# Loads at the start, banks of the hidden sums, and the order of the last outer product in a Strassen FFN kernel

## The chip, the cores and the metric

The kernel runs on one core of one Trainium2 chip. The metric is the device time of a run in microseconds; three runs of the kernel before gave a median of 1380.54 us (1380.38 to 1381.13). One further execution was recorded by the hardware profiler; its trace and the page made from it are what is read here. The engines are PE (TensorE, with its weight loads as PEld), DVE (VectorE), ACT (ScalarE), POOL (GpSimd) and SP (SyncE, which issues most transfers).

## What is computed

```python
def cond(x, condition, weights):           # x (32, 64, 1024)
    W = weights[condition]                 # (32, 64, 64), gathered
    return jnp.einsum('bct,bcd->bdt', x, W)

def ffn(input, inter_w, inter_b, output_w, output_b):   # D = 1024, F = 4096
    h = gelu(jnp.einsum('bsd,df->bsf', input, inter_w) + inter_b)
    return jnp.einsum('bsf,fd->bsd', h, output_w) + output_b

x = x + ffn(cond(x, itok_B_0_15, cond_weights), ...)
```

All of it is in fp32. The 32 rows of x are first mixed with a small matrix each, which is picked by an index; the result goes through two large matrix products with a gelu between, and x is added at the end.

## The kernel before

**Two levels of Strassen.** Each of the two large products is done by a Strassen-Winograd scheme of two levels. Layer one ("f") has eight iterations `it`, each with seven outer products; layer two ("z") has seven outer products `o` (`OUTER`, order 1, 2, 6, 7, 4, 5, 3), each with seven middle products (`MID`, order 1, 2, 5, 6, 4, 7, 3). Each of these blocks is seven inner products (`INNER`), which are issued as matmuls of 128x256 and accumulate in PSUM. One inner product is eight matmul records.

**PSUM.** Pool `pst` has two buffers of one bank (tag "t"). Pool `psacc` has tags A, B and C, two buffers each. In a block the inner products come in slots: 0 in A, 1 in B, 2 in C, 3 in A, 5 in C, 6 in A and 11 (that is, slot 4 of the next block) in A. VectorE reads each product and adds it to running sums in SBUF (`add`, line 181).

**The order is written by hand.** Every piece of work is entered as `at(time, function, ...)`, and the list is issued in the order of these times. One unit is one inner product; a block takes 7 units and an iteration or outer product 49. Each engine runs its instructions in the order of issue.

**Start.** x comes in pairs of rows, 16 in all; ten of them are mixed at the start and six later. `FIRST = (2, 3, 6, 7, 0, 1, 4, 5)` and then 8 and 9 is the order. `load_x` issues a load on SP (line 275), `gather` fetches the small matrices with POOL, `mix` runs 16 small matmuls (32 records, tile py, line 308), and `mixed` copies py to SBUF by ScalarE (L331) and VectorE (L333). xpool has six buffers. The last two of `FIRST`, 4 and 5, go to a buffer of another pool. On SP the loads stand in the order x2, x3, x6, x7, w11, x0, x1, x4, x5, w12, x8, x9, w21, w22, b1, where wij is a quarter of 1 MB of the first layer's weights. POOL makes sums of the weights (wi, ws) from them, and VectorE sums of y. Before the first mix, `warm` runs matmuls on zeros.

**After gelu.** From iteration 4 on, `hidden` also makes sums of the four parts of a gelu result. For the inner ones `inner_s1_copy` copies half of a part to PSUM by ScalarE (`to_psum`, L200), and `inner_s1` adds it by VectorE. The PSUM tile is of tag "B", which fB uses in slot 1 of each block. There are 16 such hidden blocks with four copies each.

**The last outer product.** In layer two, `product3` and `read3` do the inner products and their additions to the middle sums mD, mX, mY, mZ (`MID_STATE`). A result that is done (`MID_DONE`) goes to the outer sums, is transposed by PE (tile tp, L1006), added to x (`load_xb`, L996) and stored (`store_out`, L1017). `mid_w`, `mid_h`, `mid_s3`, `inner_w2` and `inner_h2` prepare operands on POOL and VectorE ahead of each block. In outer product 6, which is the last, the results of the last middle products go straight to the output, by `add_copy`, `ends_in` and the transposes.

Of the kernel before, what the change touches and what calls it, by code (L numbers as in the profile page):

```python
# [9 lines left out]
F32 = mybir.dt.float32  # L10
# [53 lines left out]
}  # L64
MID_DONE = {2: (("D", (0, 0)),), 7: (("X", (1, 1)), ("Y", (1, 0))), 3: (("Z", (0, 1)),)}
MID_SUM = 6


@with_exitstack
def kernel(  # L70
# [101 lines left out]
    def at(time, fn, *args):  # L172
        steps.append((time, len(steps), fn, args))
# [20 lines left out]
    def to_psum(src, tag=None):  # L194
        uid[0] += 1
        pool = late["acc"] if tag else pst
        t = pool.tile([P, 2, W], F32, tag=tag or "t", name=f"t{uid[0]}")
        if len(src.shape) == 2:
            t = t.rearrange("p k n -> p (k n)")[:, : src.shape[1]]
        nc.scalar.copy(t, src)  # L200
        return t

# [63 lines left out]
    FIRST = (2, 3, 6, 7, 0, 1, 4, 5)  # L266

    def load_x(i):
        if i in FIRST[6:]:
            if "x" not in XT:  # L270
                XT["x"] = misc.tile([P, 2, T], F32, tag="m8", name="x0_m")
            XT[i] = XT["x"][:, FIRST.index(i) - 6, :]
        else:
            XT[i] = xpool.tile([P, T], F32, tag="x0", name=f"x0_{i}")
        nc.sync.dma_start(XT[i], x_rows[i])

    def warm():
# [276 lines left out]
    S1 = {}  # L554

    def inner_s1_copy(it, fin, sub):
        S1[it, fin, sub] = to_psum(H[it, fin, sub][:, 1, :], "B")

    def inner_s1(it, fin, sub):

# [113 lines left out]
    t0 = -len(order) * MIX - 0.7  # L674
    for j, i in enumerate(order):
        t = t0 + j * MIX
        at(-40 + 0.1 * j if j < 8 else t0 + (j - 6) * MIX + 1.5, load_x, i)
        at(t, mix, i)
        at(t + MIX + 0.4, mixed, i)
    at(t0 + 10 * MIX + 1, store_y1, 8)  # L680
    at(-39.65, load_w1, 0, "11")
    at(-38, load_w1, 0, "12")
    at(t0 + 3 * MIX + 1.7, load_w1, 0, "21")
    at(t0 + 3 * MIX + 1.8, load_w1, 0, "22")
    at(-1, lambda: nc.sync.dma_start(b1, inter_b.rearrange("(f p) -> p f", p=P)))
    at(t0 + 10 * MIX + 0.42, end_mix)
    ty = t0 + 4 * MIX + 1.5
# [24 lines left out]
    for it in range(nit):  # L712
        a, s = divmod(it, NG)
        b0 = 49 * it
        if it > 0:
            for n, t in W_LOAD.items():
                at(b0 - 49 + t, load_w1, it, n)
        for n, t in W_AT.items():
            if it == 0:
                t = {1: -10, 2: -8, "s3": -4, "s1": -3}.get(n, t)  # L720
            if isinstance(n, str):
                at(b0 + t, outer_w1, it, n)
            else:
                at(b0 + t, inner_w1, it, n)
        for o, p in enumerate(OUTER):
            b = b0 + 7 * o
            plan_block(
                b, 1, 7 * it + o, (it, p), "f", mm1,
                lambda l, r, it=it, p=p, a=a: (WI[it, p][l], YI[a, p][r]),
            )  # L730
            fin = STATE[p][1]
            if fin is not None:
                hidden(b, it, fin)
            if it == NG:
                at(b - 49 + 13, load_y1, Y_ORDER[o])
                right_sums(b - 49 + 20, lambda p=p: inner_y(1, p), gap=0.8)
        pieces = []
        if it == 1:
            for k in range(KQ):
                e = {}  # L740
                t = b0 + 5 + 10.8 * k
                at(t, load_piece, k, e)
                right_sums(t + 5, lambda k=k, e=e: piece_targets(k, e), gap=0.8)
                at(t + 10.5, store_piece, k, e)
        elif it >= 2:
            n = -(-len(w2_pieces) // (nit - 2))
            for j in range(n):
                i = (it - 2) * n + j
                if i < len(w2_pieces):
                    e = {}  # L750
                    t = b0 + 9.5 + 14 * j
                    pc = w2_pieces[i]
                    at(t - 6, load_w2, pc, e)
                    at(t - 2.5, early_t1, pc, e)
                    at(t + 0.6, store_w2, pc, e, ("11", "21", "22"))
                    right_sums(t, lambda pc=pc, e=e: w2_targets(pc, e), gap=0.8)
                    at(t + 5, store_w2, pc, e, ("t1", "t2", "t3", "t4"))
# [55 lines left out]
    def mid_s3(time, o, t):  # L813

        e = {}

        def one(k):
            if k == 0:
                HT[o, "s3", t] = yq.tile([P, NG, 2, W], F32, tag="yq", name=f"hs3_{o}_{t}")
            e[k] = to_psum(HT[o, "s2", t][:, k])  # L820

        def two(k):
            add(nc.vector, HT[o, "s3", t][:, k], HT[o, "22", t][:, k], e[k], sub=True)

        for k in range(NG):
            at(time + 0.8 * k, one, k)
            at(time + 0.8 * k + 0.6, two, k)
# [35 lines left out]
    def inner_h2(time, o, q):  # L863
# [15 lines left out]
        for k in range(2):  # L879
# [4 lines left out]
            at(t + 1.9, sub, "s4", "12", "s2", k)  # L884
            at(t + 2.2, sub, "s3", "22", "s2", k)

    MS = {}
    OS = {}
    b2c = lambda n2, n1, n0: late["b2"][:, 4 * n2 + 2 * n1 + n0 : 4 * n2 + 2 * n1 + n0 + 1]
# [1 line left out]

    def product3(o, i, r):
        _, p, bank, start, _ = r
        q = MID[i]
        if start:
            acc3[o, i, bank] = late["acc"].tile(
                [P, 2, W], F32, tag=bank, name=f"z{bank}{o}{i}"
            )[:, 0, :]
        mm3(acc3[o, i, bank], win(o, q, RIGHT[p]), hin(o, q, LEFT[p]), start)
# [6 lines left out]

    def read3(o, i, r):
        _, _, bank, _, (t, n0) = r
        q = MID[i]
        acc = acc3[o, i, bank]  # L910
        for tgt, src in MID_STATE[q]:
            first = (o, i, tgt, t, n0) not in seen
            seen.add((o, i, tgt, t, n0))
            m = pair(o, tgt, t)[:, n0, :]
            if first and src is None:
                nc.scalar.copy(m, acc)  # L916
            elif first:
                add(nc.vector, m, acc, MS[o, src, t][:, n0, :])
            else:
                add(nc.vector, m, acc, m)  # L920
# [93 lines left out]
    def store_out(o, blk, t, n0s=(0, 1), eng=nc.sync):  # L1014
# [19 lines left out]
    )  # L1034
    for o in range(7):
        b = end1 + 49 * o
        pick = lambda later, first: b + (first if o == 0 else later)
        for (n, t), tt in H_LOAD.items():
            at(pick(*tt), load_h, o, n, t)
        for n, tt in W_LOAD2.items():  # L1040
            at(pick(*tt), load_w, o, n)
        for n, k, *tt in POOL2:
            if n == "w":
                at(pick(*tt), inner_w2, o, MID[k])
            elif n[0] == "t":
                at(pick(*tt), mid_w, o, n)
            else:
                at(pick(*tt), mid_h, o, n, k)
        mid_s3(b + 24, o, 0)
        mid_s3(b + 28, o, 1)  # L1050
        for i, q in enumerate(MID):
            bq = b + 7 * i
            inner_h2(bq - 2.2 if (o, i) != (0, 0) else bq + 0.7, o, q)
            rs = INNER
            if (o, i) == (6, 6):

                at(bq + 7.01, read3, o, i, (6, 7, "A", False, (1, 0)))
                rs = INNER[:-1] + ((7, 4, "B", True, (1, 0)),)
            for r in rs:
                at(bq + r[0], product3, o, i, r)  # L1060
                at(bq + r[0] + 1, read3, o, i, r)
            if q == MID_SUM:
                for t in range(2):
                    add_copy(
                        bq + (7.1, 12.1)[t],
                        lambda o=o, t=t: MS[o, "Z", t], lambda o=o, t=t: MS[o, "X", t],
                    )
            for j, (src, mb) in enumerate(MID_DONE.get(q, ())):
                for t in range(2):
                    if (o, i) == (6, 6):  # L1070

                        add_copy(
                            bq + (1.2, 4.45)[t],
                            lambda o=o, t=t: MS[o, "Z", t],
                            lambda mb=mb, t=t: OS["X", mb, t],
                        )
                        at(bq + 6.3, ends_in, o, mb, t)
                    f = bq + (7.1, 12.2)[t] + j
                    if (o, i) != (6, 6):
                        at(f, outer_copy, o, src, mb, t)  # L1080
                        at(f + 0.7, outer3, o, src, mb, t)
                    if STATE[OUTER[o]][1] is None:
                        continue
                    at(b + 38 if (o, mb, t) in ENDS else f - 1.8, load_xb, o, mb, t)
                    if (o, i) == (6, 6):
                        continue
                    at(f + 2.2, transpose, o, mb, t)
                    at(f + 3.2, add_x, o, mb, t)
                    at(f + 4, store_out, o, mb, t)
# [52 lines left out]
```

## Time and profile before

| | |
|---|---|
| runs, median of 3 | 1380.54 us (1380.38 to 1381.13) |
| profiled execution, time | 1380.57 us |
| profiled execution, span | 1378.8 us |
| mean granted clock of TensorE | 0.985 |
| bytes moved by DMA | 273.40 MB, mean 198 GB/s |

Busy times on the page are sums over one execution. An engine's "idle before" is time in which it stood still before instructions of a group, and the name behind the arrow is what released it. A granted clock of 0.5 means that TensorE ran at half speed. A few matmul records can be missing from a trace. Names such as fA or zB are the PSUM tiles of the two layers by bank; fD, fV and fX are sums in layer one, mX, mY and mZ in layer two.

### The profile page before, as it was taken

Reading aid. Unit: us, or ns where it says so; the run is one execution under the profiler, and the core shown is the slowest. Engines: PE = TensorE matmul, PEld = TensorE weight load, DVE = VectorE, ACT = ScalarE, POOL = GpSimd, SP = SyncE. Lnnn points to the kernel's source line nnn. Section 1 sums busy time; section 2 is a strip of 40 time slices with the busy share of each in tenths; the row PEclk is TensorE's granted clock in tenths of the full one; section 3 lists DMA queues with packets and bytes.
Section 4 is the critical chain, followed back from the end, with each engine's and each line's share of the span. In section 5 each row is a group of like instructions: output and inputs, shape, how many; then the busy total and the mean of one; then the engine's idle time right before and its main releaser. Section 6 shows DMA issues by size and latency. Waiting matters only on the chain.

```text
span 1378.8 us, 18997 instructions
## 1 busy us (share of the span) xinstructions
PE 1353.6 (98%) x6568; PEld 1184.9 (86%) x6568; DVE 883.4 (64%) x1579; ACT 487.5 (35%) x984; POOL 961.4 (70%) x601
## 2 busy tenths in 40 slices
PE   9999999999999999999999999999999999999998
PEld 8988888888888788788788888888888888888886
DVE  1656557575687755756657575675766757767675
ACT  1533324234254442532524332432333333333241
POOL 7462854958659477496672985958959689595791
PEclk7799999999999999999999999999999999999999
DMA  8255578686897757676668327074270723907511
GB/s 285 71 169 200 172 224 285 215 279 223 285 358 267 247 189 252 228 229 223 227 206 294 111 92 290 19 292 163 89 278 3 285 103 112 357 28 268 204 51 57
DMA packets 135216, 273.40 MB, mean 198 GB/s; under 512 B 15440, under 2 KB 67920, under 8 KB 123472
## 3 DMA queue, kind: packets, MB, share of 16 engines
q1 hardware_dynamic: 134336, 271.53, 57.0%
q8 instruction: 53, 0.87, 0.3%
q0 software_dynamic: 512, 0.53, 0.1%
q14 instruction: 43, 0.35, 0.1%
q10 hardware_dynamic: 272, 0.13, 0.0%
HBM read 167.28 MB, written 104.86 MB: 197 GB/s over the span
## 4 chain that ended last, share of the span: by engine, by line
PE 92%; DVE 4%; ACT 1%; issue 1%; DMA 1%; POOL 0%; DVEq 0%; ACTq 0%
PE fA L525 26%; PE zA L536 23%; PE fC L525 13%; PE zC L536 12%; PE fB L525 7%; PE zB L536 6%; PE py L308 2%; DVE hs L181 1%; PE tp L1006 1%; PE warm L286 1%; PE pl L308 1%; ACT t L200 1%; DMA y<-y_d 1%; DVE fX L181 1%; DVE fV L181 1%
## 5 line engine op out<-in xcount | busy, mean ns | idle before, releaser
L525 PE MATMUL fA<-yi,wi 128*128 128x256 f32 x896 | 212.5, 380 | 2.2 <-DVE fD L181 0.8
L181 DVE TENSOR_TENSOR hs<-h,t 128x512 f32<-128x512 f32 x308 | 199.8, 678 | 7.1 <-ACT t L200 3.4
L536 PE MATMUL zA<-hs,wt 128*128 128x256 f32 x840 | 198.1, 379 | 0.0
L181 POOL TENSOR_TENSOR h<-h,h 128x1024 f32<-128x1024 f32 x84 | 196.1, 2361 | 0.6 <-DMA h<-hs_d 0.6
L525 PEld LDWEIGHTS fA<-yi,wi 128*128 128x128 f32 x896 | 169.4, 190 | 27.7 <-DVE fX L181 1.9
L536 PEld LDWEIGHTS zA<-hs,wt 128*128 128x128 f32 x840 | 158.6, 190 | 20.9
L181 POOL TENSOR_TENSOR ws<-w,w 128x1024 f32<-128x1024 f32 x32 | 74.8, 2360 | 75.2 <-PE fA L525 75.1
L550 ACT ACTIVATE fD<-fD,b 128x256 f32<-128x256 f32 x128 | 57.9, 500 | 187.5 <-DVE fD L181 186.7
L181 POOL TENSOR_TENSOR wi<-w 128x512 f32<-128x512 f32 x80 | 101.7, 1271 | 30.5 <-PE fC L525 24.6
L200 ACT COPY t<-h 128x512 f32<-128x512 f32 x140 | 81.9, 590 | 82.4 <-DVE hs L181 78.2
L200 ACT COPY t<-hs 128x512 f32<-128x512 f32 x112 | 65.4, 588 | 113.6 <-DVE hs L181 113.6
L181 POOL TENSOR_TENSOR wt<-v 128x512 f32<-128x512 f32 x35 | 44.5, 1272 | 82.2 <-DMA v<-w_d 78.4
L181 DVE TENSOR_TENSOR fX<-fA,fX 128x512 f32<-128x512 f32 x104 | 71.3, 685 | 47.0 <-PE fA L525 46.7
L181 POOL TENSOR_TENSOR wi<-w,wi 128x512 f32<-128x512 f32 x40 | 50.8, 1271 | 61.7 <-PE fA L525 55.0
L525 PE MATMUL fC<-y,wi 128*128 128x256 f32 x384 | 91.0, 380 | 0.1
L525 PEld LDWEIGHTS fC<-y,wi 128*128 128x128 f32 x384 | 72.7, 190 | 10.4 <-issue 0.5
L536 PE MATMUL zC<-hs,v 128*128 128x256 f32 x336 | 79.5, 379 | 1.3 <-ACT mX L916 1.3
L536 PE MATMUL zA<-h,wt 128*128 128x256 f32 x328 | 77.5, 379 | 0.0
L525 PE MATMUL fA<-yi,w 128*128 128x256 f32 x320 | 75.6, 379 | 0.0
L536 PEld LDWEIGHTS zC<-hs,v 128*128 128x128 f32 x336 | 63.8, 190 | 10.3 <-ACT mX L916 1.7
L525 PE MATMUL fB<-y,w 128*128 128x256 f32 x256 | 63.6, 393 | 7.9 <-DVE fV L181 7.9
L536 PEld LDWEIGHTS zA<-h,wt 128*128 128x128 f32 x328 | 62.3, 190 | 8.5
(178 smaller groups left out, 2820.6 us busy)
## 6 DMA issues: line engine op xcount, KB each, us to landing
h<-hs_d SPq DMA_DIRECT2D x56, 1024.0 KB, 6.9
w<-in_L_ffn_inter_w_dram SPq DMA_DIRECT2D x32, 1024.0 KB, 6.7
hs_d<-hs SPq DMA_DIRECT2D x96, 256.0 KB, 3.1
v<-w_d SPq DMA_DIRECT2D x21, 1024.0 KB, 10.8
hs_d<-fD SPq DMA_DIRECT2D x64, 256.0 KB, 5.7
w2p<-in_L_ffn_output_w_dram SPq DMA_DIRECT2D x32, 512.0 KB, 5.7
w_d<-w2p SPq DMA_DIRECT2D x64, 256.0 KB, 2.8
w_d<-w2t SPq DMA_DIRECT2D x48, 256.0 KB, 6.6
```

Of the source, the lines that this page charges most:

```text
L181: eng.tensor_tensor(o, a, b, ALU.subtract if sub else ALU.add)
L200: nc.scalar.copy(t, src)
L286: nc.tensor.matmul(t[:, :W], z[:, :P], z[:, P:], start=True, stop=True)
L308: nc.tensor.matmul(out[j][:, k, :], XT[i][half, ts(k, P)], wsel(i)[half, :], start=True, stop=True,)
L525: nc.tensor.matmul(acc[:, u, :], lt[:, k, ts(u, P)], rt[:, k, :], start=start and u == 0 and k == 0, stop=k == 1, skip_group_check=True,)
L536: nc.tensor.matmul(acc, wl[:, k, :], hr[:, k, :], start=start and k == 0, stop=k == NG - 1, skip_group_check=True,)
L550: nc.scalar.activation(t[:, u, :], t[:, u, :], AF.Gelu_apprx_tanh, bias=b1[:, f : f + 1])
L1006: nc.tensor.transpose(tp[:, v, ts(n0, P)], d[:, n0, ts(v, P)], late["ident"])
```

## The change

It has three parts.

1. At the start, all ten x tiles come from xpool. Six x loads and w11 (after them) are issued first. The loads of pairs 4, 5, 8 and 9 follow when the mixes of 2, 3, 6 and 7 have freed a buffer; w12, w21 and w22 are issued after those. `inner_w1(0, 2)` gets a later time.
2. The copies of gelu's sums use tag "C" in place of "B".
3. In outer product 6 the middle products come in the order 1, 2, 5, 6, 7, 4, 3, with a state E in place of X for the result (1, 1). `mid_s3` is about five units earlier, POOL's work has an order of its own, one addition after middle product 6 is split in two, one operand tile (hs3_(6,1)) comes from another pool, and the loads of x and the last additions are earlier.

```diff
+MID_END = (1, 2, 5, 6, 7, 4, 3)
+MID_STATE_END = {**MID_STATE, 7: (("E", "Z"), ("X", "X")), 4: (("X", "X"),)}
+MID_DONE_END = {
+    2: (("D", (0, 0)),), 7: (("E", (1, 1)),), 4: (("X", (1, 0)),), 3: (("Z", (0, 1)),),
+}
...
     def load_x(i):
-        if i in FIRST[6:]:
-            if "x" not in XT:
-                XT["x"] = misc.tile([P, 2, T], F32, tag="m8", name="x0_m")
-            XT[i] = XT["x"][:, FIRST.index(i) - 6, :]
-        else:
-            XT[i] = xpool.tile([P, T], F32, tag="x0", name=f"x0_{i}")
+        XT[i] = xpool.tile([P, T], F32, tag="x0", name=f"x0_{i}")
         nc.sync.dma_start(XT[i], x_rows[i])
...
     def inner_s1_copy(it, fin, sub):
-        S1[it, fin, sub] = to_psum(H[it, fin, sub][:, 1, :], "B")
+        S1[it, fin, sub] = to_psum(H[it, fin, sub][:, 1, :], "C")
...
-        at(-40 + 0.1 * j if j < 8 else t0 + (j - 6) * MIX + 1.5, load_x, i)
+        at(-40 + 0.1 * j if j < 6 else t0 + (j - 6) * MIX + 1.5, load_x, i)
...
-    at(-39.65, load_w1, 0, "11")
-    at(-38, load_w1, 0, "12")
-    at(t0 + 3 * MIX + 1.7, load_w1, 0, "21")
-    at(t0 + 3 * MIX + 1.8, load_w1, 0, "22")
+    at(-39.45, load_w1, 0, "11")
+    for j, n in enumerate(("12", "21", "22")):
+        at(t0 + 3 * MIX + 1.6 + 0.1 * j, load_w1, 0, n)
...
-                t = {1: -10, 2: -8, "s3": -4, "s1": -3}.get(n, t)
+                t = {1: -10, 2: -6.8, "s3": -4, "s1": -3}.get(n, t)
...
+                pool, tag = (wpool, "w") if (o, t) == (6, 1) else (yq, "yq")
+                HT[o, "s3", t] = pool.tile([P, NG, 2, W], F32, tag=tag, name=f"hs3_{o}_{t}")
...
+    POOL2_END = POOL2[:9] + (
+        ("t3", 0, 21.1), ("w", 4, 23.8), ("t4", 0, 26), ("w", 5, 28.7), ("s4", 0, 30.9),
+        ("s4", 1, 33.6), ("w", 6, 36.3),
+    )
...
-        mid_s3(b + 24, o, 0)
-        mid_s3(b + 28, o, 1)
-        for i, q in enumerate(MID):
+        mid_s3(b + (18.9 if o == 6 else 24), o, 0)
+        mid_s3(b + (22.2 if o == 6 else 28), o, 1)
+        for i, q in enumerate(mids(o)):
...
-            if (o, i) == (6, 6):
+            if (o, i) in ((6, 5), (6, 6)):
...
                     add_copy(
-                        bq + (7.1, 12.1)[t],
-                        lambda o=o, t=t: MS[o, "Z", t], lambda o=o, t=t: MS[o, "X", t],
+                        bq + f,
+                        lambda o=o, t=t, c=c: MS[o, "Z", t][:, c, :],
+                        lambda o=o, t=t, c=c: MS[o, "X", t][:, c, :],
                     )
...
-                            bq + (1.2, 4.45)[t],
+                            bq + (1.2, 2.3)[t],
...
-                        at(bq + 6.3, ends_in, o, mb, t)
+                        at(bq + 4, ends_in, o, mb, t)
...
-                    at(b + 38 if (o, mb, t) in ENDS else f - 1.8, load_xb, o, mb, t)
+                    at(b + 33 if (o, mb, t) in ENDS else f - 1.8, load_xb, o, mb, t)
```

More of the change, by code (lines that the diff above doesn't have):

```diff
@@ L198, in to_psum @@
         if len(src.shape) == 2:
-            t = t.rearrange("p k n -> p (k n)")[:, : src.shape[1]]
+            t = t.rearrange("p k n -> p (k n)")
+        t = t[:, : src.shape[1]]
         nc.scalar.copy(t, src)
@@ L818, in one @@
             if k == 0:
-                HT[o, "s3", t] = yq.tile([P, NG, 2, W], F32, tag="yq", name=f"hs3_{o}_{t}")
+                pool, tag = (wpool, "w") if (o, t) == (6, 1) else (yq, "yq")
+                HT[o, "s3", t] = pool.tile([P, NG, 2, W], F32, tag=tag, name=f"hs3_{o}_{t}")
             e[k] = to_psum(HT[o, "s2", t][:, k])
@@ L885, in inner_h2, with mids @@
             at(t + 2.2, sub, "s3", "22", "s2", k)
+    def mids(o):
+        return MID_END if o == 6 else MID
     MS = {}
@@ L893, in product3 @@
         _, p, bank, start, _ = r
-        q = MID[i]
+        q = mids(o)[i]
         if start:
@@ L908, in read3 @@
         _, _, bank, _, (t, n0) = r
-        q = MID[i]
+        q = mids(o)[i]
         acc = acc3[o, i, bank]
-        for tgt, src in MID_STATE[q]:
+        for tgt, src in (MID_STATE_END if o == 6 else MID_STATE)[q]:
             first = (o, i, tgt, t, n0) not in seen
@@ L1034 @@
     )
+    POOL2_END = POOL2[:9] + (
+        ("t3", 0, 21.1), ("w", 4, 23.8), ("t4", 0, 26), ("w", 5, 28.7), ("s4", 0, 30.9),
+        ("s4", 1, 33.6), ("w", 6, 36.3),
+    )
     for o in range(7):
         b = end1 + 49 * o
-        pick = lambda later, first: b + (first if o == 0 else later)
+        pick = lambda later, first=None: b + (first if o == 0 else later)
         for (n, t), tt in H_LOAD.items():
@@ L1041 @@
             at(pick(*tt), load_w, o, n)
-        for n, k, *tt in POOL2:
+        for n, k, *tt in POOL2_END if o == 6 else POOL2:
             if n == "w":
-                at(pick(*tt), inner_w2, o, MID[k])
+                at(pick(*tt), inner_w2, o, mids(o)[k])
             elif n[0] == "t":
@@ L1062 @@
             if q == MID_SUM:
-                for t in range(2):
+                parts = ((0, slice(0, 2), 7.1), (1, slice(0, 2), 12.1))
+                if o == 6:
+                    parts = (parts[0], (1, slice(1, 2), 7.2), (1, slice(0, 1), 12.1))
+                for t, c, f in parts:
                     add_copy(
-                        bq + (7.1, 12.1)[t],
-                        lambda o=o, t=t: MS[o, "Z", t], lambda o=o, t=t: MS[o, "X", t],
+                        bq + f,
+                        lambda o=o, t=t, c=c: MS[o, "Z", t][:, c, :],
+                        lambda o=o, t=t, c=c: MS[o, "X", t][:, c, :],
                     )
-            for j, (src, mb) in enumerate(MID_DONE.get(q, ())):
+            for j, (src, mb) in enumerate((MID_DONE_END if o == 6 else MID_DONE).get(q, ())):
                 for t in range(2):
@@ L1076 @@
                         )
-                        at(bq + 6.3, ends_in, o, mb, t)
-                    f = bq + (7.1, 12.2)[t] + j
+                        at(bq + 4, ends_in, o, mb, t)
+                    f = bq + (7.1, 8.1 if (o, i) == (6, 5) else 12.2)[t] + j
                     if (o, i) != (6, 6):
```

## The prediction

> **What bounds the kernel now.** I read the page's shares first, then the chain of waits, the granted clock by stage, the waits by engine, and last the timeline at each place the change touches.
>
> ```profile
> PE   1353.6 (98%) x6568; PEld 1184.9 (86%) x6568; DVE 883.4 (64%) x1579; ACT 487.5 (35%) x984; POOL 961.4 (70%) x601
> PE 92%; DVE 4%; ACT 1%; issue 1%; DMA 1%; POOL 0%; DVEq 0%; ACTq 0%
> ```
>
> TensorE is busy for 98% of the span and is 92% of the chain: the kernel is one string of matmuls. An edit is worth time only where it closes a hole in that string or raises its clock. A record of 128x256 takes 0.216 us of PE at full clock (8 records of one inner product in 1.73 us) and 0.427 at half. The change leaves the number of matmuls alone. So I look for holes and for slow clock.
>
> Start, by windows (duration, busy time and count of PE, PEld, DVE, ACT, POOL; then the granted clock, DMA share and GB/s):
>
> ```profile
> 14.30:16.70 2.40, 2.40 (x39) 2.30 (x39) 0.00 (x0) 0.00 (x0) 1.79 (x3) 1.00 1.03 386
> 16.70:19.20 2.50, 0.75 (x7) 0.49 (x6) 0.00 (x0) 0.00 (x0) 2.36 (x3) 1.00 1.02 373
> 19.20:48.50 29.30, 29.30 (x277) 29.23 (x277) 13.05 (x28) 10.06 (x26) 23.27 (x14) 0.51 0.46 134
> 48.50:53.80 5.30, 5.30 (x13) 4.21 (x13) 3.24 (x6) 3.16 (x7) 0.00 (x0) 0.50 0.59 189
> ```
>
> The ten mixes (320 records) begin at full clock, nearly stop at 16.7, and then run 29.3 us at half clock, as do the first products. The slices show no other slow stretch of this length. The timeline of the stop:
>
> ```profile
> 17.77 0.21 PE L308 MATMUL py<-wsel_e,x 64*128 64x64 f32 x1 [0.98 <-issue]
> 18.48 0.43 PE L308 MATMUL py<-wsel_e,x 64*128 64x64 f32 x3 [0.49 <-issue]
> 19.19 1.29 PE L308 MATMUL py<-wsel_e,x 64*128 64x64 f32 x14 [0.28 <-issue]
> 19.38 0.65 ACT L331 COPY y<-py 128x256 f32<-128x256 f32 x2 [17.36 <-remote]
> ```
>
> No data wait is named: PE waits on "issue", and ScalarE sees the end of the first mix only at 19.38. All of it lies inside the stretch in which the DMA engines are full.
>
> Layer one, waits by engine (total, times, longest), and then PE's timeline at one such place:
>
> ```profile
> PE fB L525 <- DVE fV L181: 7.9, 4, 2.5
> ```
>
> ```profile
> 476.36 1.96 PE L525 MATMUL fA<-y,w 128*128 128x256 f32 x8
> 480.77 3.55 PE L525 MATMUL fB<-y,w 128*128 128x256 f32 x8 [2.45 <-DVE fV L181]
> 484.15 1.03 PE L525 MATMUL fC<-y,w 128*128 128x256 f32 x4
> ```
>
> Product fB waits for the VectorE addition that frees its bank, and then runs at half clock (3.55 us for 8 records). The tail, by timeline:
>
> ```profile
> 1370.46 0.60 PE L1006 MATMUL tp<-ident,mZ 128*128 128x128 f32 x4
> 1371.85 0.66 PE L1006 MATMUL tp<-ident,mX 128*128 128x128 f32 x4 [0.79 <-DVE xe L181]
> 1373.29 0.66 PE L1006 MATMUL tp<-ident,mY 128*128 128x128 f32 x4 [0.57 <-DVE xe L181]
> ```
>
> After the last product three rounds of transpose and addition follow each other.
>
> **What the Trainium skill says.** (1) "TensorE: Matmul & The Clock Gate", Part 1: the clock is halved after an idle window of about 3.4 us, restored after a busy one, and the windows run free of the kernel. The trace agrees: half clock lies in 19.82 to 53.95 and 480.62 to 484.03, which is ten windows and one of 3.413 us on one grid. (2) The same page, "Why this matters for your kernels", allows holes up to about 3 us. Here the hole of 2.45 us at 478 did cost the clock and one of 2.46 at 567.5 did not; position on the grid decides. (3) "DMA: Bandwidth & Descriptors", "Where 436 GB/s comes from", puts HBM at about 358 and the fabric at 435 GB/s; the trace has 373 to 393 GB/s with a share over 1, so the start is full. (4) "PSUM — Partial Sum Buffer", "The four PSUM rules": 8 banks of 512 fp32. Two "t" tiles and two each of A, B, C use all 8, so the copies can change banks, not gain one. No run here shows that count itself.
>
> **Part 1, the start.** It removes nothing from PE. The loads listed before any wait fall from eight x of 0.52 MB, w11 and w12 of 1.05 (6.29 MB) to six x and w11 (4.19 MB). x4, x5, x8 and x9 now stand in SP's queue behind the mixes that free their buffers, and w12, w21, w22 and b1 stand behind those. At 390 GB/s from 4.5 us the listed bytes end at about 15.3 instead of 20.6. Two prices follow.
> The hole: the PE time lost between about 16.6 and 19.2 is some 2.6 us. If full DMA queues cause it, it goes, since they drain before. The profile names no cause, so this is a guess; bounds 0 and -2.6.
> The clock: mixes cost 0.056 us per record at full rate (the spacing before the hole) and 29.3/277 = 0.106 at half. At half clock PE was busy without a break for 29 us and the clock did not return, while 5.3 us of fA and fB restored it. So these small 64x64 matmuls seem to count little as activity, and I take it that they do not hold the clock either: it falls at 19.82 (the grid) or one window later. Until 19.82 PE then does (19.82-14.3)/0.056 = 98 records, where it did about 50: 48 x 0.106 = 5.1 us. One window more adds 3.41/0.056 - 3.41/0.106 = 29 records, 3.1 us. So -5.1 to -8.2; I take -6.5. If the clock holds to the end: all mixes take 320 x 0.056 = 18 us and end at 32.5, then fA and fB at full clock; 48.6 - 32.5 = 16 and 2.5 for the first 12 records at half clock, less a microsecond for supply, about -17.5.
> Late next: x4 at about 20, w12 about 27.7 instead of 23.2, and with it POOL's wi2 (28 to 33 instead of 23 to 28) and the sums behind it, s2 at 47. Block two wants its operand at about 58, so these are covered; with the hole kept, POOL is some 10 us later but needs the operand at 78. Four x loads behind mixes stay ahead of the seventh mix even at 1.8 us a mix.
>
> **Part 2, banks of the copies.** The number of copies (16 hidden blocks of four) and of additions (0.41 us) is unchanged; they now hold a C bank. What waits is fC, one product (1.73 us) after fB. The chain at 478 ends with VectorE's fV at 480.71. fB will start at 476.36 + 1.73 = 478.1; fC is wanted at 479.8 and gets its bank at 480.7: a hole of 0.9, too short to halve the clock by what the other holes show (the grid window around 567 was still busy for nearly half and kept it; this one is busy for three quarters). Before, fC began at 484.15. Gain 3.4. At 567.5 and 657 the same hole without clock loss: 2.6 - 0.9 = 1.7 each. Five smaller holes before fB (0.25 each at 494, 582 and 672; 0.96 at 607.6; 0.85 at 744.6) vanish, being shorter than one product. Sum 3.4 + 3.4 + 0.75 + 1.8 = 9.4, less 0.25 which a hole at 603, paced by VectorE, takes back: -9.1, bounds -6 and -10.
>
> **Part 3, the last outer product.** The order moves the products that feed mX and mY ahead, so that only mZ is left after the last one. Out of the tail go two transposes of four (0.6 each) and two rounds with VectorE (0.69 each and the waits). Counted from the start of the last zA of block 5 (1342.66): the last zB ends at 15 x 1.727 + 4 x 0.44 = +27.7 against +27.9 now (which has a hole of 1.1 in it); the last store is issued at +30.2 against +32.9. One more VectorE addition and one more copy of half size lie in their own slack. Against it: mid_s3 is earlier, so four additions of 0.6 us stand before a read on VectorE at about 1320.4, which then ends at 1323.2 with 1323.7 needed. That is covered by half a microsecond only. -2.4, bounds -3 and -1. POOL's new order is ready 3 us or more ahead of each use.
>
> **A bystander.** At 1279 a hole of 2.6 us ends in one half-clock window (1282.75 to 1286.17). The hole stays; with everything earlier by an amount that is no multiple of 3.413 it most likely falls differently on the grid: -1.2, bounds 0 and -1.4.
>
> **Sum.** The profiled execution took 1380.57 (span 1378.8, 1.8 around it), the median 1380.54, so both serve alike. 1380.5 - 9.1 - 2.4 - 1.2 = 1367.8 without the start; with -6.5 it is 1361.3.
>
> **The rivals.**
> R1, the hole at 16.6 stays, since it isn't the DMA that makes it (PE ran at full speed inside full queues from 4.5 to 16.6, which speaks for it; that it ended as the queues emptied speaks against): 1367.8. The lower bounds of parts 2 and 3 would make it 1372.
> R2, the mixes hold the clock: -17.5 for the start, 1350.3. For it: they ran at 1.00 until 16.7, and one busy PE without holes is what the clock asks for; against it: 29 us of them never raised it.
> R3, slower: the C banks are no freer than the B banks. The copies now take turns with fC's own accumulators, and VectorE, busy through 475 to 482, sets when they come free. If every hidden block gets a new hole of w and the old ones gain nothing, the time is 1380.5 - 2.4 - 1.2 - 6.5 + 16w = 1370.4 + 16w: slower from w = 0.63, and 1386 at w = 1. Against it: each copy is asked for after the previous fC was read, and the wait starts one product later.
>
> **How the numbers follow.** Forecast (clock falls at 19.82 or 23.2) 0.38; R1 0.32; R2 0.24; R3 0.06. The range 1350 to 1369 holds the first three but for their edges; it leaves out R3 and the weaker part of R1 on one side, and the better part of R2 on the other. The change can be told from nothing from 0.2% on (2.8 us). Only R3 is slower, 0.05, with 0.02 for a tie; the rest is faster, 0.93.
>
> **What would show it.** Start: no PE gap at 16 to 19, the time at which the clock first falls, the start of the first fA (48.6 before; 40 to 43.5 forecast, 32.5 in R2, 48.6 in R1). Banks: the row of fB waiting for fV gone, three gaps of about 0.9 before fC, no half clock near 480. Tail: only mZ transposed after the last product, store 2.5 us after it. I am wrong if fC shows waits in most hidden blocks, or if PE starves for wi2 or s2 before 60 us.

## The result and the profile after

The changed kernel took 1366.88 us (median of four, 1366.11 to 1367.58), the kernel before beside it 1380.68: a ratio of 0.990 with a 95% interval of 0.9882 to 0.9917, 13.8 us less. The forecast was 1361; the time is that of rival R1 (1367.8). The profiled execution took 1367.58 with a span of 1365.8, 13.0 us less than the one of before.

Both traces have 6568 matmul records, so the same record number is the same piece of work, and the difference of its start times in the two traces says where time was won:

| matmul record (counted from 0) | before, us | after, us | difference | what lies between this row and the one above |
|---|---|---|---|---|
| 416 | 61.63 | 61.79 | +0.17 | the start |
| 2400 | 464.22 | 464.42 | +0.20 | first half of layer one |
| 4000 | 824.79 | 816.25 | -8.54 | hidden sums in bank C |
| 6100 | 1271.08 | 1262.55 | -8.53 | most of layer two |
| 6200 | 1295.07 | 1284.88 | -10.20 | the half-clock window near 1283 |
| end of span | 1378.80 | 1365.78 | -13.02 | the last outer product |

In these two traces part 1 won nothing (+0.2), part 2 8.7 us, the window 1.7 and part 3 2.8. The page's shares after, in the order shown for before:

```profile
PE   1347.9 (99%) x6568; PEld 1182.9 (87%) x6568; DVE 883.3 (65%) x1581; ACT 488.9 (36%) x985; POOL 962.0 (70%) x601
PE 92%; DVE 4%; issue 1%; ACT 1%; POOL 1%; DMA 1%; DVEq 0%; ACTq 0%
```

The start by windows, with the columns as before (after the duration the busy time and count of PE, PEld, DVE, ACT, POOL, then clock, DMA share, GB/s):

```profile
14.30:16.70 2.40, 1.78 (x32) 1.83 (x30) 0.00 (x0) 0.00 (x0) 1.79 (x3) 1.00 0.39 131
16.70:19.20 2.50, 0.44 (x3) 0.48 (x3) 0.00 (x0) 0.00 (x0) 2.35 (x3) 0.96 0.12 33
19.20:48.50 29.30, 29.20 (x275) 29.19 (x275) 12.65 (x28) 10.10 (x26) 15.07 (x10) 0.50 0.60 181
48.50:53.80 5.30, 5.30 (x22) 4.40 (x21) 3.65 (x7) 2.18 (x5) 5.30 (x4) 0.56 0.40 139
```

The DMA share between 16.7 and 19.2 fell from 1.02 to 0.12, as it was meant to, and the hole is still there: 3 records in 2.5 us. The clock then falls and stays at half to the end of the mixes. Full DMA queues were not what made the hole.

Layer one, the wait after (the line of fB and fV shown for before is gone from PE's waits), and PE's timeline at the place shown for before:

```profile
PE fC L527 <- DVE fV L187: 2.5, 3, 0.8
```

```profile
476.57 1.96 PE L527 MATMUL fA<-y,w 128*128 128x256 f32 x8
478.37 1.89 PE L527 MATMUL fB<-y,w 128*128 128x256 f32 x8
481.08 1.97 PE L527 MATMUL fC<-y,w 128*128 128x256 f32 x8 [0.83 <-DVE fV L187]
482.89 1.89 PE L527 MATMUL fA<-yi,wi 128*128 128x256 f32 x8
```

The wait is one product later, in fC, and what was 2.45 is 0.83. The clock stays this time: eight records of fB take 1.89 us in place of 3.55. There are three such waits in the whole layer, and none in the other hidden blocks.

The tail by timeline:

```profile
1358.31 1.89 PE L538 MATMUL zB<-h,wt 128*128 128x256 f32 x8
1360.04 0.60 PE L1011 MATMUL tp<-ident,mZ 128*128 128x128 f32 x4
1361.42 0.77 PE L1011 MATMUL tp<-ident,mZ 128*128 128x128 f32 x4 [0.78 <-DVE xe L187]
1362.35 0.42 ACTq L1022 DMA_DIRECT2D out_dram<-xe  x1
```

Only mZ is transposed after the last product, and the last store is issued 2.3 us after the first of these transposes began; before, the transposes of mX and mY came between. The hole at the seam of the last two outer products, by windows, first before and then after:

```profile
1279.20:1281.70 2.50, 0.28 (x3) 0.04 (x1) 2.50 (x6) 0.00 (x0) 0.00 (x0) 1.00 1.06 398
1282.70:1286.10 3.40, 3.40 (x12) 2.74 (x11) 0.35 (x1) 0.37 (x1) 0.00 (x0) 0.50 0.99 386
```

```profile
1270.50:1273.20 2.70, 0.48 (x3) 0.07 (x2) 2.70 (x6) 0.00 (x0) 0.09 (x1) 1.00 1.06 392
1273.20:1277.00 3.80, 3.80 (x22) 3.42 (x23) 1.61 (x3) 0.37 (x1) 0.00 (x0) 1.00 1.02 330
```

The hole itself is unchanged (2.6 us from start to start of its records in both), but this time no half-clock window follows. The traces show a pattern. In each of them the changes of the clock lie whole multiples of 3.413 us apart: before, it rose at 53.87, fell at 480.54 and fell again at 1282.67, which are 125 and 235 such steps. They form a grid of windows. PE is idle for 2.2 us of this hole. Before, all of that lay in one window (1279.25 to 1282.67), PE was busy for 35% of it, and the clock halved at its end. After, two windows shared the hole, busy for 76% and 57%, and the clock stayed. All fourteen traces of this study have this hole and fit: in six it lay whole in one window and the clock halved behind it; in eight it was split, the emptier window was still busy for 42% or more, and the clock stayed. The line therefore lies between 35% and 42% in these runs.

### The profile page after: what moved, and what is told of

It reads as the page before. It is cut to its first block, busy times and chain, and to the rows that moved or that the text cites. A ratio compares the mean times of both kernels' runs of the same rounds, so it can differ in the third digit from the quotient of the medians.

```text
span 1365.8 us, 19025 instructions
## 1 busy us (share of the span) xinstructions
PE 1347.9 (99%) x6568; PEld 1182.9 (87%) x6568; DVE 883.3 (65%) x1581; ACT 488.9 (36%) x985; POOL 962.0 (70%) x601
## 4 chain that ended last, share of the span: by engine, by line
PE 92%; DVE 4%; issue 1%; ACT 1%; POOL 1%; DMA 1%; DVEq 0%; ACTq 0%
PE fA L527 26%; PE zA L538 24%; PE fC L527 13%; PE zC L538 12%; PE fB L527 6%; PE zB L538 6%; PE py L310 2%; PE tp L1011 1%; DVE hs L187 1%; PE warm L288 1%; PE pl L310 1%; POOL w2p L187 1%; DVE fX L187 1%; DVE fV L187 0%; DMA hs_d<-fD 0%
## 5 line engine op out<-in xcount | busy, mean ns | idle before, releaser
L538 PEld LDWEIGHTS zA<-hs,wt 128*128 128x128 f32 x840 | 158.4, 190 | 20.9
L187 POOL TENSOR_TENSOR wt<-v,wt 128x512 f32<-128x512 f32 x35 | 44.5, 1272 | 33.7 <-PE zA L538 33.7
```

The lines of the kernel that those rows point to most:

```text
L187: eng.tensor_tensor(o, a, b, ALU.subtract if sub else ALU.add)
L538: nc.tensor.matmul(acc, wl[:, k, :], hr[:, k, :], start=start and k == 0, stop=k == NG - 1, skip_group_check=True,)
```

## The experiments

**Each part alone.** The parts were put into the kernel before one at a time; each diff is the part of that name in the change shown above.

> Only part 1 (the start) is made. Theory (the hole in the mixes does not come from full DMA queues, so fewer listed loads win nothing): 1380.6, within 0.6 of before, hole of about 3 us before 19.3 as in both kernels. Rival (the start cost something that the other parts hide): more than 1 us slower.

```diff
-        at(-40 + 0.1 * j if j < 8 else t0 + (j - 6) * MIX + 1.5, load_x, i)
+        at(-40 + 0.1 * j if j < 6 else t0 + (j - 6) * MIX + 1.5, load_x, i)
...
```

> Only part 2 (tag C) is made. Theory (the trace of the changed kernel, by equal record numbers, has 8.7 us of gain between 464 and 825 us): 1380.6 - 8.7 = 1371.9, and the half-clock window near 480 is gone. If the window near 1283 moves as well, 1.7 more: 1370.2. Rival (the gain at 464 to 825 needs the new start): under 4 us.

```diff
-        S1[it, fin, sub] = to_psum(H[it, fin, sub][:, 1, :], "B")
+        S1[it, fin, sub] = to_psum(H[it, fin, sub][:, 1, :], "C")
...
```

> Only part 3 (last outer product) is made. Theory: 1380.6 - 2.8 = 1377.8, all of it after 1340 us, with the half-clock window near 1283 still there. Rival (part 3 works through VectorE's backlog at 1279): the hole of 2.6 us there changes.

```diff
-        for i, q in enumerate(MID):
+        for i, q in enumerate(mids(o)):
...
```

| kernel | median, us | ratio to before (1380.48) | 95% interval |
|---|---|---|---|
| part 1 alone | 1379.55 (12 runs) | 1.0001 | 0.9992 to 1.0010 |
| part 2 alone | 1369.74 (4 runs) | 0.9925 | 0.9906 to 0.9944 |
| part 3 alone | 1377.46 (18 runs) | 0.9977 | 0.9970 to 0.9984 |

Part 1 is worth nothing, part 2 about 10.7 (8.8 in its trace at record 4000 counted from record 416, and 1.7 at the window near 1283, which moved too), part 3 about 3.0. They add up to the change. The ratios are those of the record and not quotients of the two medians (for part 1 that would be 0.9993). The profiled execution of part 1 was 3 us quicker than that of before, and its trace says why: no half-clock window fell at 480, and the one at the start ended a window earlier (30.7 us of half clock in place of 34.1). At 480 nothing in the program differs. At the start it does, but the same difference shows between two executions of the changed kernel (34.1 us of half clock in its trace, 30.7 in that of its repetition below), so part 1 need not be its cause. Such luck is why 29 executions of the kernel before spread from 1377.3 to 1381.6, and why a part of 1 us needs many runs.

**Is the hole tied to a number of instructions, a moment, or the clock's windows?** Fewer matmuls on zeros let the mixes start sooner.

```diff
-            for _ in range(12):
+            for _ in range(8):
```

> The changed kernel with 16 instead of 24 matmuls on zeros before the first mix, so that the mixes can start 3.4 us sooner (10.9 instead of 14.3). What makes the hole in the mixes? Theory 'moment' (something else on the chip holds PE until about 19.3): the hole still ends at 19.2 to 19.4 and is longer; the time stays within 1 us. Rival 'count' (PE's instructions run short after a fixed number of them): the hole starts 8 matmuls later in the mixes, at about record 67 of the mixes instead of 35 to 39, near 14.5 us. Rival 'grid' (it starts with a window of the clock gate): it starts at a multiple of 3.413 us before the fall of the clock, wherever the mixes are.

It took 1365.62 us (ratio 0.9895, 0.9876 to 0.9914), 1.3 less than the changed kernel on the first chip. The mixes started at 12.1, the hole at 15.0, and it ended only at 19.8. So its length isn't fixed: it ends at about the same moment wherever the mixes begin. It doesn't begin with a window of the clock either (the fall came at 16.70, so a window began at 13.29). The figure 67 in the expectation was a slip of mine: eight matmuls are 16 records, so "count" asked for record 51 to 55 of the mixes. The first pause came after 49. "Count" was therefore still alive.

```diff
-            for _ in range(12):
+            for j in range((36, 14)[n]):
+                c = (8, W)[n]
                 nc.tensor.matmul(
-                    t[:, :W], z[:, :P], z[:, P:], start=True, stop=True
+                    t[:, :c], z[:, :P], z[:, P : P + c], start=True, stop=True
```

> The changed kernel, with the 24 matmuls on zeros (256 columns) replaced by 36 of 8 columns and then 14 of 256, so that PE has issued 50 matmuls (100 records) before the first mix in about the same time. In five traces so far the hole starts when PE has issued 84 to 88 matmul records, weight loads not counted. Theory 'count': the hole moves into the last of the big matmuls on zeros, and no hole lies in the mixes. Then it also shows whether mixes hold the clock: if they do, the first fA starts near 34 us and the time is about 1353; if they do not, the clock falls at the second or third window after the mixes begin, and the time is 1359 to 1366. Rival 'moment': the hole ends at 19.1 to 19.8 in the mixes as in all traces so far, and the time stays within 2 us of the changed kernel.

The short matmuls took 0.21 us a record, as long as the long ones at full clock; the clock did not rise before 20.3, which drew out the long ones behind them, and the mixes began only at 24.7. They had no hole, ran all 320 records in 18.1 us at full clock, and the kernel took 1361.36 (ratio 0.9871, 0.9854 to 0.9887) in spite of the late start.

```diff
-            for _ in range(12):
+            for _ in range(18):
```

> The changed kernel with 36 instead of 24 matmuls on zeros, so that the mixes start near 19.5 us. Theory 'count': the hole is there all the same, after 8 of the matmuls of the first mix (16 of its records), near 20.4 us. Rival 'moment': the mixes start after 19.3 and have no hole.

> The kernel of warm36 again, timed: the mixes start at 19.04 us, when the gathers are done, and keep the clock. 1357.3 as in the single run if that was typical; up to 3 us more if a half-clock window falls on one of the holes in some executions. Rival (the single run was a lucky one): 1362 or more.

PE's timeline of this kernel (start, duration, engine, line, operation):

```profile
1.33 17.78 PE L288 MATMUL warm<-zeros 128*128 128x256 f32 x72 [1.33 <-DVE zeros L283]
19.04 18.08 PE L310 MATMUL py<-wsel_e,x 64*128 64x64 f32 x320
37.05 1.99 PE L527 MATMUL fA<-y,w 128*128 128x256 f32 x8
```

No hole after 16 records: "count" fell as the only cause. Mixes that start after 19 run through at full clock. As part of the cause it did not fall. In all eight traces of the study that have the hole, it begins when PE has done 81 to 90 of its records, matmuls on zeros included (the expectation above said 84 to 88), while the time varies from 15.0 to 16.6 us. In the kernel with short matmuls and in this one PE reached its 84th record only at 20.9 and 19.7 us, when whatever ends at 19 was over. So neither run separates "held from a moment on" from "held from a number of records on, if that comes before 19".

Waiting five microseconds longer made the kernel about 9 us faster than the changed one: 1357.33 in one run, and 1357.77 (four runs) in a later measurement. That one was on a chip where the kernel before took 1363.63 (seven runs, ratio 0.9954, 0.9937 to 0.9970) and not 1380. No trace of the kernel before was taken there, but its mean granted clock was 0.997 and not 0.985. At half clock that leaves some 8 us (2 x 0.003 x 1362) in place of 41 (2 x 0.015 x 1379), and the mixes alone had 34. So on that chip ten gathers in a row did not cost the mixes their clock. Whether they still made a hole, a shorter one or none, no run shows.

**What ends at 19?** Of the engines, only GpSimd is at work during the hole: it issues ten indirect gathers, 1.25 us apart, the last from 16.5 to 17.4, and then begins its sums. From the changed kernel's timeline:

```profile
16.47 0.94 POOL L263 DMA_INDIRECT wsel_e<-in_L_cond_weights_dram,rows  x1 [0.30 <-issue]
17.20 0.44 PE L310 MATMUL py<-wsel_e,x 64*128 64x64 f32 x3 [1.12 <-issue]
19.30 4.98 PE L310 MATMUL py<-wsel_e,x 64*128 64x64 f32 x45 [1.67 <-issue]
```

The next two kernels change the number of gathers. In the first, six are left out and the mixes read four matrices in place of ten, so its output is not the right one; in the second four more are read into a tile that nobody uses. Each ran once.

```diff
     def wsel(i):
+        if i in (0, 1, 4, 5, 8, 9):
+            i = {0: 2, 1: 3, 4: 6, 5: 7, 8: 2, 9: 3}[i]
...
-    for j, i in enumerate(order):
+    for j, i in enumerate(order[:4]):
         at(-50 + 0.1 * j, gather, i)
```

> The changed kernel with only the first four of the ten gathers (six are left out; the other mixes read the four matrices that are there). GpSimd then issues its last gather at 8.8 us instead of 16.5. Theory 'gathers' (PE's matmuls on gathered matrices are held while gathers are under way, until about 1.8 us after the last one was issued): no hole in the mixes, full clock to their end, first fA near 32.5 us, 1352 or less. Rival 'moment': the hole still ends at 19.1 to 19.8 and the clock falls, 1366 to 1368.

```diff
...
         at(-50 + 0.1 * j, gather, i)
+    for j in range(4):
+        at(-48 + 0.1 * j, gather_more, j)
```

> The changed kernel with four more gathers behind the ten, into a tile that nobody reads. GpSimd's last gather is issued 5 us later, near 21.5 us. Theory 'gathers': the hole lasts until about 24 us, and GpSimd's sums come 5 us later. Rival 'moment': the hole ends at 19.1 to 19.8.

With four gathers, 1351.41 us; its last gather, then windows (columns as above):

```profile
8.92 0.94 POOL L265 DMA_INDIRECT wsel_e<-in_L_cond_weights_dram,rows  x1 [0.30 <-issue]
```

```profile
14.30:16.70 2.40, 2.40 (x37) 2.07 (x37) 0.00 (x0) 0.00 (x0) 0.86 (x1) 1.00 0.19 70
16.70:19.20 2.50, 2.50 (x50) 2.50 (x48) 0.76 (x2) 1.24 (x4) 2.34 (x3) 1.00 0.46 133
19.20:32.40 13.20, 13.20 (x242) 13.20 (x239) 9.45 (x21) 7.13 (x19) 3.43 (x4) 1.00 0.94 318
```

With fourteen, 1371.74 us; timeline:

```profile
18.43 0.29 PEld L319 LDWEIGHTS py<-wsel_e,x 64*128 64x128 f32 x3 [1.23 <-issue]
...
21.39 0.95 POOL L273 DMA_INDIRECT wsel_x<-in_L_cond_weights_dram,rows  x1 [0.30 <-issue]
...
24.79 5.60 PE L319 MATMUL py<-wsel_e,x 64*128 64x64 f32 x50 [0.46 <-issue]
24.90 2.20 SPq L286 DMA_DIRECT2D x<-in_x_dram  x2
24.91 0.65 ACT L342 COPY y<-py 128x256 f32<-128x256 f32 x2 [22.89 <-remote]
```

With the last gather issued at 8.9, there is no hole at all and full clock, even in the stretch with a DMA share of 0.94. With the last gather over at 22.3, the mixes crawl (one to three records at a time, 0.7 us or a multiple of it apart) until 24.8, and ScalarE and SP learn of the first finished mix only then. The end of the hole follows the end of the run of gathers, not the moment and not the DMA load. The extra gathers write a tile that no matmul reads, so it isn't a wait for their data. Nor does the landing of the gathers end it: in the trace of before, 64 of the 320 packets of the ten gathers moved after 19.25, when the hole was over. What inside the chip holds the matmuls back was not shown. A shortage of PE's instructions after 81 to 90 records, while gathers run, is not excluded: with four gathers PE passed that number at 16.7, long after the last one.

**A complete kernel without the hole.** Six or seven gathers are left in a row, the others each go behind one of the first sums on GpSimd.

From the one with seven:

```diff
-    for j, i in enumerate(order):
+    for j, i in enumerate(order[:7]):
         at(-50 + 0.1 * j, gather, i)
...
+            late_gathers = iter(order[7:] if (it, p) == (0, 1) else ())
             pool_add(s1, lblk(q, 1, 0), lblk(q, 1, 1))
+            for i in late_gathers:
+                gather(i)
+                break
             pool_add(s2, s1, lblk(q, 0, 0), sub=True)
...
```

> The changed kernel with six of the ten gathers in a row, as before, and each of the last four behind one of the four first sums (wi) on GpSimd, after w11 has landed near 15.8 us. The result is complete again. Theory (a run of gathers holds the mixes until about 2 us after its last one; one gather alone is short enough to be covered): no hole after about 14.9, the mixes keep the clock, first fA between 32.5 and 34.5 us, 1351 to 1354. Rival (each gather holds the mixes as long as it runs): holes near 17 to 26 us, the clock falls, and the time is 1364 or more.

> Seven gathers in a row and three singly behind sums on GpSimd, so that the ninth mix no longer waits for its matrix (2.05 us at 27.8, with half clock behind it, in the run with six). 1350 to 1352 on either sort of chip if single gathers are covered; if the run of gathers holds the mixes to 16 us and the clock falls, 1362 or more.

> The changed kernel once more, beside the kernel before on one chip. In the last call the kernel before took 1363.6 us and not 1380, 17 us less, which is what the mixes lose with the hole and the half clock. If this chip is of that sort: no fall of the clock in the mixes, the changed kernel near 1350 to 1352, the gain of 12 to 13 us as on the first chip (parts 2 and 3 and the window near 1283), and no more for part 1. If it is of the first sort: 1366 to 1368 against 1380, hole and fall as before.

The one with six took 1353.77 us, on the chip where the kernel before took 1363.63 (ratio 0.9928, 0.9911 to 0.9944), so it couldn't tell the two theories apart; its ninth mix waited 1.78 us for its matrix (2.05 from start to start), and the clock fell behind that. The one with seven ran on a chip where the kernel before takes 1380, beside the kernel before (1381.06) and the changed kernel (1366.50, ratio 0.9901, 0.9884 to 0.9917). It took 1352.88: ratio to before 0.9805, 0.9789 to 0.9822, and 13.6 us less than the change, a little above the 1350 to 1352 that were expected. The ten gathers are all there, so this pair on one chip is the cleanest sign that the unbroken row of ten costs the time. Its PE and GpSimd, by timeline:

```profile
13.59 18.08 PE L310 MATMUL py<-wsel_e,x 64*128 64x64 f32 x320
31.61 1.99 PE L539 MATMUL fA<-y,w 128*128 128x256 f32 x8
35.29 0.89 PE L539 MATMUL fB<-y,w 128*128 128x256 f32 x3 [1.69 <-DVE ys L335]
```

```profile
12.71 0.94 POOL L263 DMA_INDIRECT wsel_e<-in_L_cond_weights_dram,rows  x1 [0.30 <-issue]
16.00 1.27 POOL L187 TENSOR_TENSOR wi<-w 128x512 f32<-128x512 f32 x1 [2.34 <-DMA w<-in_L_ffn_inter_w_dram]
17.41 0.97 POOL L263 DMA_INDIRECT wsel_e<-in_L_cond_weights_dram,rows  x1
...
19.83 0.97 POOL L263 DMA_INDIRECT wsel_e<-in_L_cond_weights_dram,rows  x1 [0.16 <-issue]
...
22.25 0.97 POOL L263 DMA_INDIRECT wsel_e<-in_L_cond_weights_dram,rows  x1 [0.16 <-issue]
```

The row of seven ends at 13.65, and PE reaches its 84th record at 15.6. Then three gathers run beside the mixes, 2.4 us apart, and the mixes neither stop nor lose their clock. What is late next is VectorE's copy of ys (1.7 us before fB). This is the fastest complete kernel of the study.

## Why the prediction held, and where its steps failed

The time fell inside the range, but in R1's place and not the forecast's, 5.9 us above it: the range held because it was wide enough for the rival, not because the forecast of the start was right.

*Part 1.* The forecast took -6.5 and +0.2 was measured. Two steps failed. "If full DMA queues cause it, it goes": the queues drained (share 0.12 in place of 1.02) and the hole stayed; it goes when the run of gathers ends earlier. The prediction called this a guess; R1 had the right evidence, that PE had run at full speed inside full queues up to 16.6. And "I take it that they do not hold the clock either" was wrong the other way: without a hole, 320 records ran at full clock for 18 us (three complete kernels and the one with four gathers). The clock fell because of the hole, not because the matmuls are small. That they never raised it from half clock in 29 us is true, and didn't carry over. R2's sum was therefore about right for a start without the hole: it said 1350.3; it was 1351.4 with four gathers and 1352.9 in the complete kernel. The trace of before has the first fall at 19.74 and not at 19.82; no sum depends on that.

*Part 2.* -9.1 forecast, -8.7 measured, by the mechanism described: three waits of 0.83 remain before fC (0.9 said), the half-clock window near 480 is gone, the smaller holes too. The hole paced by VectorE at 603 (597.8 after) grew from 1.21 to 1.49, for which 0.25 had been set aside. R3 asked for waits in most hidden blocks; there were three, 2.5 us in sum. Of the 8.7 us, 1.7 are that half-clock window, which the trace of part 1 alone, with the banks as before, didn't have either: that much is luck of the execution.

*Part 3.* -2.4 forecast, -2.8 measured; the tail is as told, and the tight read on VectorE cost no visible hole.

*The bystander.* -1.2 forecast, -1.7 measured, which is luck that the forecast had weighed. Whether it is won is a matter of where the hole falls on the clock's windows: in the kernels with 36 matmuls on zeros and with seven gathers in a row a half-clock window came back behind the same hole.

*Supply.* GpSimd's wi2 began at 36.7, 13 us later than before (10 were foreseen with the hole kept), and nothing waited for it.

Without part 1 the steps said 1367.8: 0.9 from the measured median.

## What to carry to other kernels

When PE stands still on "issue" and no wait is named, look for what the other engines do in that stretch and change that, before blaming the busiest resource: here the DMA share was 1.02 beside the hole, and with 0.12 the hole was still there. A small hole is worth its length and the clock behind it: with the hole of some 3 us the kernel took 1366.5, without it 1352.9 on the same chip. In this kernel it paid to let the copies borrow the bank that is wanted one product later.

## What the runs showed of the hardware

- On the chips that were traced with it, a run of indirect gathers on GpSimd, 1.25 us apart, held up TensorE's mixes until about 2 us after the last gather (19.1 to 19.8 with ten, 24.8 with fourteen, no hole with four), and hid their completion from ScalarE and SP for as long. The hole began after 81 to 90 of PE's records. Single gathers 2.4 us apart, each with a sum between, did not hold the mixes up. The matmuls on zeros ran through the same stretch, but there were only 72 to 78 of their records by 19.2 us, so that they are exempt isn't shown.
- Matmuls of 64x64 at full clock kept it for 18 us; the same ones at half clock did not bring it back in 29 us.
- A hole with 2.2 us of idle PE, near 1254 to 1282 us, cost a half-clock window when it lay in one window of the clock's grid (busy for 35%), and nothing when two windows shared it (42% or more), with the same work around it. The grid itself lies differently in each execution: the first fall came at 19.02 and at 20.59 in two of the changed kernel. "TensorE: Matmul & The Clock Gate", Part 1, says that the windows run free of the kernel, and this agrees. It speaks of an idle window; here one that was busy for 35% was enough to halve the clock.
- On one of the chips the kernel before took 1363.6 us and not 1380, at a mean clock of 0.997. Why the mixes kept their clock there is open.
